# Windowed linear attention: left and right window borders passed by half blocks of four columns instead of whole blocks of eight

## Chip, cores and metric

One core of one Trainium2 chip. Time is device microseconds of one execution; the time of a kernel is the median of its runs.

## What is computed

An image of 256 channels and 64 x 64 pixels goes through three layers. The change is in the first, a linear attention over windows, with 8 heads of 32 channels and three window sizes:

```python
q = sigmoid(Wq x);  k = sigmoid(Wk x);  v = (Wv x) / |Wv x|     # x after a group norm
Ik  = integral(k);  Ikv = integral(k v^T)                       # sums over all rows above, columns to the left
for w in (1, 2, 4):                                             # windows of 64, 32 and 16 pixels
    attn = q . box(Ikv, 64 // w)                                # sum of k v^T over a window round each pixel
    norm = q . box(Ik, 64 // w)
    outs.append(attn / (norm + 1e-6))
x = x + Wout concat(outs) + bout
```

A window that leaves the image is cut at its edge. The second layer is a causal attention over the 4096 pixels as tokens (with layer norms and two dense layers), the third a mixture of experts of which two are computed.

## The kernel before

The k v sums of a window are never formed for each pixel. The image is cut into blocks of 8 x 8 pixels. `HALF` is half a window, 8, 16 or 32 pixels; `wi` counts them. For `wi` 1 and 2 a window of a query block has three kinds of keys:

- **Inside:** whole blocks that lie in the window of all queries of a block. Their k v sums come from two-dimensional running sums over blocks, `ikv`; `states` (L480) takes differences of these for a block row Y, ScalarE spreads them to block-diagonal matrices `bd` over four heads (L498), and `inside` (L404) multiplies them with q: for each of 8 blocks and 4 heads one product with 128 rows, 32 output columns and 64 queries (L409).
- **Left and right** (`beside`, L127): key blocks n columns to the left and right, of which each query column takes some key columns. The product of keys and queries is formed, blocked pairs are set to zero, and the rest is multiplied with v. `BLOCKED` (-64) is added for them by a small bf16 product of a row table and a column table (L348), and a ReLU takes the sum to zero.
- **Above and below** (`above`, L140): the same with rows; for `wi` 0 it is the whole window.

A `Part` is one tile of 128 keys with a rectangle of query rows and columns. `packed` (L105) fills lists of up to 512 query positions with parts; a part is split at a row where the piece has at least 96 positions. `push` (L337) takes a list: mask products (L348) and score products (L357) of four heads into four PSUM banks, the four heads on four groups of 32 rows of the PE array; then ReLU copies to SBUF, 5 of 8 on ScalarE (L326), 3 of 8 on VectorE (L328). One list later `add` (L369) multiplies with v (L390, 128 rows, 32 output columns, four heads side by side) into an accumulator. Accumulators of the left-and-right pass belong to a pair (`wi`, X), with two PSUM buffers for them; `store` (L397) copies a full one and writes it to HBM, and the up-and-down pass loads it by rows (L669) and adds it in `finish` (L415).

All this is done for each half of the heads (`hg` 0 and 1). A half goes through:

- four strips of 16 image rows: `project` (q and k, and k's running sum along rows), `values` (v, and its way to HBM and back in row order as `vh`), and from the second strip on `block_sums` (L580) of the strip before: k v sums of each block, 8 blocks x 2 x 4 heads as products of 64 keys;
- the left-and-right pass (L632 to L659), with `block_sums` of the last strip behind its first list;
- the up-and-down pass (L665 to L690): for each block row Y its lists, with `states`, `boxes` and `norms` (window sums of k and their product with q, for the next Y), `spread_norms`, `convolve` of Y-1, and in the second half `causal.norm` and `causal.turn` of Y-1 (layer norm of tokens for the second layer) at fixed places of the list's count.

What sets the order: inside `tc.manual_schedule` the instructions of PE and GpSimd run in the order in which the program issues them; for ScalarE, VectorE and the DMA queues a scheduler orders them[...]. GpSimd's order during the left-and-right pass is written out at L636 to L654: running sums of `ikv`, running sums of `ik` over 64 rows, `boxes(0)`, the reordering of k to `kh`, and for `hg` 0 the addition of a bias to the tokens `t`; `boxes(1)` follows from the loop over Y.

In the second layer `behind` (L921) forms sums over tokens, in tiles that `Causal.load` (L800) takes from the memory of `ik`; the rows of 128 queries are taken from the last to the first, with the dense layers' steps of finished groups (`later`) put between their products by `one()` (L1108 to L1148).

## Time and profile before

| what | us |
|---|---|
| median of 3 runs | 2015.45 (2014.27 to 2017.11) |
| the profiled execution's own time | 2017.58 |
| its span, first to last instruction | 2015.9 |
| strips, first half of the heads (41 to 92.7) | 51.7 |
| left-and-right pass, first half (92.7 to 203.6) | 110.9 |
| up-and-down pass, first half (203.6 to 516) | 312.4 |
| strips, second half (516 to 577.9) | 61.9 |
| left-and-right pass, second half (577.9 to 689) | 111.1 |
| up-and-down pass, second half (689 to 1032) | 343.0 |
| causal attention (1032 to 1748) | 716.0 |
| its end and the choice of experts (1748 to 1788) | 40.0 |
| experts (1788 to 2016) | 228.0 |

Engines are PE (TensorE; PEld its weight loads), DVE (VectorE), ACT (ScalarE), POOL (GpSimd) and SP (SyncE, which only issues DMAs here). "L390" is line 390 of the kernel. A row of the timeline has the start in us, the time until the last of its instructions ends, engine, line, operation, the tiles written and read, their shapes and the count; in square brackets the idle time of the engine before it and what ended that. Of a product, "32\*128 32x192" means weights of 32 rows and 128 columns with 192 columns moving. Consecutive rows of PE overlap[...]: the next row's start tells when the array took it. In a row of a group, the count is followed by busy time, the mean time of one in ns, and idle time before.

### The profile page before, as it was taken

To read this page: it belongs to the slowest core of one execution; us is meant where nothing else is said; L and a number is where in the kernel's file an instruction comes from. 1 tells how busy PE (TensorE), PEld (TensorE's weight loads), DVE (VectorE), ACT (ScalarE), POOL (GpSimd) and SP (SyncE) were. 2 spreads that over 40 slices of the span, in tenths; PEclk is the share of its full clock that TensorE was granted. 3 is DMA by queue.
4 is the path that set the end of the run, shared out by engine and by line. 5 is a ranking of instruction groups with operands and counts; after the bars stand their busy time and mean duration, and the time that the engine had idled before them with its cause. 6 is when DMAs were issued, how large, how long until landed. Compare 5 with 4: busy or idle time off the path is not lost.

```text
span 2015.9 us, 46364 instructions
## 1 busy us (share of the span) xinstructions
PE 1862.9 (92%) x20326; PEld 1224.0 (61%) x20326; DVE 985.5 (49%) x2190; ACT 829.0 (41%) x1459; POOL 431.2 (21%) x709
## 2 busy tenths in 40 slices
PE   4999899999999999898899999999999999879998
PEld 2655565555665565555574765666666666547787
DVE  4644444544554465555463434554554555433343
ACT  0566555554356654554413323332333233223322
POOL 1384322232155122333110000000000000021220
PEclk9999999999999999999999999999999999979999
DMA  7211000000331100000200000000000000010000
GB/s 239 80 52 50 23 13 16 15 18 13 96 98 40 44 18 13 18 13 12 49 2 0 0 1 0 1 1 0 1 0 1 0 1 0 1 42 21 21 21 21
DMA packets 66891, 53.35 MB, mean 26 GB/s; under 512 B 37568, under 2 KB 56792, under 8 KB 66688
## 3 DMA queue, kind: packets, MB, share of 16 engines
q1 hardware_dynamic: 57296, 31.87, 5.8%
q10 hardware_dynamic: 8128, 14.67, 2.1%
q0 software_dynamic: 1264, 3.84, 0.6%
q8 instruction: 159, 2.61, 0.5%
q14 instruction: 44, 0.36, 0.1%
HBM read 32.93 MB, written 17.44 MB: 25 GB/s over the span
## 4 chain that ended last, share of the span: by engine, by line
PE 42%; DVE 6%; ACT 3%; issue 2%; POOL 0%; ACTq 0%; DVEq 0%; POOLq 0%
PE po L1000 11%; PE pa L956 9%; PE ph L1260 6%; PE py L1280 5%; PE pt L986 2%; PE pm L1057 1%; PE acc L390 1%; PE pm L1067 1%; PE ps L357 1%; PE ps L507 1%; DVE lnst L704 1%; DVE sT L989 1%; DVE nbs L964 1%; PE pm L916 1%; ACT s L969 1%
## 5 line engine op out<-in xcount | busy, mean ns | idle before, releaser
L326 ACT ACTIVATE pm<-ps 128x512 f32<-128x512 f32 (+19 forms) x734 | 362.6, 559 | 320.3 <-issue 164.9
L328 DVE TENSOR_SCALAR pm<-ps 128x512 f32<-128x512 f32 (+23 forms) x442 | 267.8, 636 | 291.6 <-PE ps L357 210.8
L390 PE MATMUL acc<-pm,vh 128*32 128x248 f32 (+22 forms) x3424 | 220.1, 359 | 19.8 <-DVE pm L328 19.6
L357 PE MATMUL ps<-q,kh 32*128 32x248 f32 (+23 forms) x3424 | 209.8, 360 | 0.0
L956 PE MATMUL pa<-k,qT 128*128 128x512 f32 (+3 forms) x416 | 180.2, 574 | 7.1 <-ACT qT L918 5.7
L348 PE MATMUL ps<-table,table 32*128 32x192 bf16 (+19 forms) x2512 | 146.1, 262 | 39.3 <-DVE pm L328 18.4
L989 DVE COPY sT<-pt 128x512 f32<-128x512 f32 (+3 forms) x144 | 92.7, 643 | 138.1 <-PE pt L986 137.9
L348 PEld LDWEIGHTS <-table 32*128 32x128 bf16 x2512 | 51.0, 92 | 179.7 <-issue 172.8
L390 PEld LDWEIGHTS acc<-pm,vh 128*32 128x32 f32 x3424 | 88.9, 111 | 110.3 <-issue 63.2
L357 PEld LDWEIGHTS ps<-q,kh 32*128 32x128 f32 x3424 | 146.2, 192 | 7.5 <-issue 2.7
L425 POOL TENSOR_TENSOR y<-y,rn 128x512 f32<-128x512 f32 x32 | 40.8, 1275 | 477.5 <-DVE y L424 335.0
L958 ACT ACTIVATE s<-pa,v 128x512 f32<-128x512 f32 (+3 forms) x112 | 73.8, 662 | 148.6 <-PE pa L956 148.4
L956 PEld LDWEIGHTS pa<-k,qT 128*128 128x128 f32 x416 | 75.7, 191 | 89.3 <-issue 72.4
L964 DVE TENSOR_REDUCE nbs<-s 128x1 f32<-128x512 f32 (+4 forms) x120 | 77.6, 652 | 82.7 <-ACT s L958 58.9
L1280 PE MATMUL py<-w,hT 128*128 128x256 f32 x512 | 111.8, 379 | 0.0
L1000 PE MATMUL po<-kh,sT 128*128 128x257 f32 x406 | 101.3, 390 | 9.0 <-DVE sT L989 8.9
L1280 PEld LDWEIGHTS py<-w,hT 128*128 128x128 f32 x512 | 97.3, 190 | 15.7 <-issue 1.9
L390 PE MATMUL acc<-pm,v 128*32 128x192 f32 (+11 forms) x1600 | 98.5, 360 | 2.4 <-DVE pm L328 2.4
L357 PE MATMUL ps<-q,k 32*128 32x192 f32 (+11 forms) x1600 | 98.7, 359 | 0.7 <-issue 0.7
L1000 PEld LDWEIGHTS po<-kh,sT 128*128 128x128 f32 x406 | 73.7, 193 | 22.6 <-DVE sT L989 13.8
L507 PE MATMUL ps<-l0wo,y 128*128 128x256 f32 x384 | 87.2, 384 | 0.0
L947 POOL MEMSET s<- 128x32 f32 x20 | 2.5, 125 | 376.2 <-PE pt L986 348.4
(305 smaller groups left out, 2946.2 us busy)
## 6 DMA issues: line engine op xcount, KB each, us to landing
oscratch<-ov ACTq DMA_DIRECT2D x32, 256.0 KB
ov<-oscratch SPq DMA_DIRECT2D x32, 256.0 KB
t<-in_xT SPq DMA_DIRECT2D x32, 128.0 KB
vscratch<-v SPq DMA_DIRECT2D x32, 128.0 KB
vh<-vscratch SPq DMA_DIRECT2D x16, 256.0 KB
raw<-in_x ACTq DMA_DIRECT2D x7, 512.0 KB
raw<-in_x SPq DMA_DIRECT2D x7, 512.0 KB
out<-y SPq DMA_DIRECT2D x7, 512.0 KB
```

The costliest lines, as they stand in the source:

```text
L326: nc.scalar.activation(dst, src, AF.Relu)
L328: nc.vector.tensor_scalar_max(dst, src, 0.0)
L348: nc.tensor.matmul(got[h][:, spot].rearrange("p (y x) -> p y x", y=part.r1 - part.r0), lhsT=spread[hs, int(part.vertical), :], rhs=bias[hs ...
L357: nc.tensor.matmul(got[h][:, spot].rearrange("p (y x) -> p y x", y=part.r1 - part.r0), lhsT=keys[hs], rhs=q[hs, part.r0 : part.r1, part.c0 ...
L390: nc.tensor.matmul(out, lhsT=v, rhs=pm[:, h, spot].rearrange("p (y x) -> p y x", y=part.r1 - part.r0), start=fresh, stop=(left[key] == 0), ...
L507: nc.tensor.matmul(pt[:, i * D : (i + 1) * D], lhsT=ys[wi, Y][:, (2 * j + i) * P : (2 * j + i + 1) * P], rhs=wo[:, n, :], start=(n == 0), ...
L956: nc.tensor.matmul(pp[:, 0:m], lhsT=qTs[g][:, c, i * P - g * 512 : n - g * 512], rhs=x[b // 512][c][:, 0:m], start=(c == 0), stop=(c == DC ...
L964: nc.vector.tensor_reduce(nbs[:, at : at + 1], s[:, b : b + m], AX.X, ALU.max)
L989: nc.vector.tensor_copy(sT[:, 0:full], pt[:, 0:full])
L1000: nc.tensor.matmul(acc, lhsT=sT[0:m, j * P : (j + 1) * P], rhs=rhs, start=(b == 0), stop=(m != P))
L1260: nc.tensor.matmul(ph, lhsT=w1v[:, e, c, f, :], rhs=x2[g][c], start=(c == 0), stop=(c == DC - 1))
L1280: nc.tensor.matmul(py, lhsT=hT[:, e, f, j * P : (j + 1) * P], rhs=w2v[:, e, f, :], start=(e + f == 0), stop=(e == 1 and f == FC - 1))
```

## The change

Blocks of keys of 8 x 8 are kept, but the order of pixels within a tile of 16 x 8 keys changes, so that its partitions 0 to 63 hold columns 0 to 3 and 64 to 127 columns 4 to 7. A part of the left-and-right pass then stands for two halves u: four key columns, with the four query columns that lie n blocks beside them. A tile's 128 x 8 columns of scores become 128 x 4 (three where the right side's first column has no key). What lies between moves to the inside sums, which are kept by four columns: `ikv` has 17 column places instead of 9.

- Score products: per half and head 32 rows x 64 columns of weights. Sum products: 64 rows x 32 columns, each half into an accumulator of its own, with `wi` 1 in the first 256 columns and `wi` 2 in the last. Both PSUM buffers so belong to one X. `store` makes four copies and two DMAs for each X; lists are packed for each X; parts may be split at 40 positions, in the up-and-down pass too.
- `inside`: 16 places x 4 heads, 32 rows x 32 columns of weights, 32 queries, straight from `st`; `bd` and `heads` as its scale are gone.
- `block_sums`: four quarters of 32 keys instead of two halves of 64.
- GpSimd's running sums of `ikv` come after the reordering to `kh`, and start with rows.
- The token statistics are taken at list 4 (`measure`), root and normalising at list 5.
- `after`, `sums` and `count` of the second layer leave the memory of `ik`; one query product is issued ahead of four value products; in the last large row every step is followed by a step of the dense layers.

```diff
@@ -113,7 +114,7 @@
-        if rows * (part.c1 - part.c0) >= 96:
+        if rows * (part.c1 - part.c0) >= 40:
@@ -126,15 +127,16 @@
-        c0 = 8 * X + (1 if side and X - n >= 0 else 0)
+        c0 = 8 * X + side
...
-            yield Part(wi, True, (m, kX), side, 8 * lo, 8 * hi, c0, 8 * X + 8,
-                       -8 * (2 * m - n + 1), -8 * X, (wi, X))
+            yield Part(wi, True, (m, kX), side, 8 * lo, 8 * hi, c0, 8 * X + 4,
+                       -8 * (2 * m - n + 1), -8 * X, (X,))
@@ -353,12 +357,13 @@
-            for h, hs in enumerate(hss):
-                nc.tensor.matmul(
-                    got[h][:, spot].rearrange("p (y x) -> p y x", y=part.r1 - part.r0),
-                    lhsT=keys[hs], rhs=q[hs, part.r0 : part.r1, part.c0 : part.c1],
-                    start=False, stop=(i == len(parts) - 1), skip_group_check=True,
-                )
+            for u, some in enumerate(halves if part.vertical else whole):
+                for h, hs in enumerate(hss):
+                    nc.tensor.matmul(
+                        got[h][some, spot].rearrange("p (y x) -> p y x", y=part.r1 - part.r0),
+                        lhsT=keys[hs, some], rhs=q[hs, part.r0 : part.r1, part.c0 + 4 * u : part.c1 + 4 * u],
+                        start=False, stop=(i == len(parts) - 1), skip_group_check=True,
+                    )
@@ -372,56 +377,64 @@
-                accs[key] = po.tile([P, 512], F32, name="acc")
+                accs[key] = [po.tile([P, 512], F32, name="acc") for _ in (halves if part.vertical else whole)]
...
-                    inside(group, accs[key])
+                    inside(group, accs[key][0])
...
-            for h, hs in enumerate(hss):
-                if part.vertical:
-                    out = accs[key].rearrange("p (y x) -> p y x", x=8)[
-                        hs, part.r0 : part.r1, part.c0 % 8 : part.c0 % 8 + part.c1 - part.c0]
-                    v = state["v"][:, 8 * a_ + b_, hs]
-                else:
-                    out = accs[key].rearrange("p (y x) -> p y x", x=HW)[
-                        hs, part.r0 % 8 : part.r0 % 8 + part.r1 - part.r0, part.c0 : part.c1]
-                    v = vh[:, 4 * a_ + b_, hs]
-                nc.tensor.matmul(
-                    out, lhsT=v, rhs=pm[:, h, spot].rearrange("p (y x) -> p y x", y=part.r1 - part.r0),
-                    start=fresh, stop=(left[key] == 0), skip_group_check=True,
-                )
+            for u, some in enumerate(halves if part.vertical else whole):
+                for h, hs in enumerate(hss):
+                    if part.vertical:
+                        out = accs[key][u][:, 256 * part.wi - 256 : 256 * part.wi].rearrange("p (y x) -> p y x", x=4)[
+                            hs, part.r0 : part.r1, part.c0 % 8 : part.c0 % 8 + part.c1 - part.c0]
+                        v = state["v"][some, 8 * a_ + b_, hs]
+                    else:
+                        out = accs[key][0].rearrange("p (y x) -> p y x", x=HW)[
+                            hs, part.r0 % 8 : part.r0 % 8 + part.r1 - part.r0, part.c0 : part.c1]
+                        v = vh[:, 4 * a_ + b_, hs]
+                    nc.tensor.matmul(
+                        out, lhsT=v, rhs=pm[some, h, spot].rearrange("p (y x) -> p y x", y=part.r1 - part.r0),
+                        start=fresh, stop=(left[key] == 0), skip_group_check=True,
+                    )
...
-        wi, X = group
-        o = two.tile([P, 512], F32, name="ov")
-        nc.scalar.copy(o, acc)
-        nc.scalar.dma_start(out=oscratch[wi][X], in_=o)
+        X = group[0]
+        for wi in (1, 2):
+            o = sm.tile([P, 2, 64, 4], F32, name="ov", tag="y", bufs=4)
+            c = 0 if X >= HALF[wi] // 8 else 1
+            if c:
+                nc.vector.memset(o[:, :, :, 0:1], 0.0)
+            for u in range(2):
+                nc.scalar.copy(o[:, u, :, c:], acc[u][:, 256 * wi - 256 : 256 * wi].rearrange("p (y x) -> p y x", x=4)[:, :, c:])
+            nc.scalar.dma_start(out=oscratch[wi][2 * X : 2 * X + 2].rearrange("u p n -> p u n"),
+                                in_=o.rearrange("p u y x -> p u (y x)"))
...
-        for X in range(8):
+        for X in range(16):
...
-                    acc.rearrange("p (y x) -> p y x", x=HW)[hs, :, 8 * X : 8 * X + 8],
-                    lhsT=state["bd"][wi][:, X, h, :], rhs=q[:, 8 * Y : 8 * Y + 8, 8 * X : 8 * X + 8],
+                    acc.rearrange("p (y x) -> p y x", x=HW)[hs, :, 4 * X : 4 * X + 4],
+                    lhsT=state["st"][wi][hs, X, :], rhs=q[hs, 8 * Y : 8 * Y + 8, 4 * X : 4 * X + 4],
...
-        wi, Y = group
+        (wi, Y), acc = group, acc[0]
...
-            view = lambda s: s.rearrange("p (y b x) -> p y b x", b=8, x=8)
-            nc.vector.tensor_add(view(o), view(acc), state["ov"][wi].rearrange("p b (y x) -> p y b x", x=8))
+            view = lambda s: s.rearrange("p (y b x) -> p y b x", b=16, x=4)
+            nc.vector.tensor_add(view(o), view(acc), state["ov"][wi].rearrange("p b (y x) -> p y b x", x=4))
@@ -483,20 +496,21 @@
-            rows = state["h"].tile([P, 9, 32], F32, name="srows")
-            nc.vector.tensor_sub(rows, ikv[:, min(8, Y + n), :, :], ikv[:, max(0, Y - n + 1), :, :])
-            st = state["h"].tile([P, 8, 32], F32, name="st8")
-            if n == 2:
-                nc.vector.tensor_copy(st[:, 0, :], rows[:, 2, :])
-                nc.vector.tensor_sub(st[:, 1:7, :], rows[:, 3:9, :], rows[:, 0:6, :])
-                nc.vector.tensor_sub(st[:, 7, :], rows[:, 8, :], rows[:, 6, :])
+            hi, lo = min(8, Y + n) - 1, max(0, Y - n + 1) - 1
+            rows = ikv[:, hi, :, :]
+            if lo >= 0:
+                rows = state["h"].tile([P, 17, 32], F32, name="srows")
+                nc.vector.tensor_sub(rows, ikv[:, hi, :, :], ikv[:, lo, :, :])
+            st = state["h"].tile([P, 16, 32], F32, name=f"st{wi}")
+            n *= 2
+            nc.scalar.copy(st[:, 0:n, :], rows[:, n : 2 * n, :])
+            if n == 4:
+                nc.vector.tensor_sub(st[:, n : 17 - n, :], rows[:, 2 * n : 17, :], rows[:, 1 : 18 - 2 * n, :])
+                nc.vector.tensor_sub(st[:, 17 - n :, :], rows[:, 16:17, :].to_broadcast([P, n - 1, 32]),
+                                     rows[:, 18 - 2 * n : 17 - n, :])
...
-                nc.vector.tensor_copy(st[:, 0:4, :], rows[:, 4:8, :])
-                nc.vector.tensor_sub(st[:, 4:8, :], rows[:, 8:9, :].to_broadcast([P, 4, 32]), rows[:, 1:5, :])
-            bd = state["h"].tile([P, 8, 4, 32], F32, name=f"bd{wi}")
-            for h in range(4):
-                nc.scalar.activation(bd[:, :, h, :], st, AF.Copy, scale=heads[:, 32 * h : 32 * h + 1])
-            out.append(bd)
+                nc.vector.tensor_sub(st[:, n:, :], rows[:, 16:17, :].to_broadcast([P, n, 32]), rows[:, 1 : n + 1, :])
+            out.append(st)
@@ -557,10 +571,12 @@
-                nc.sync.dma_start(
-                    out=vscratch[2 * m + s].rearrange("(y b x) j e -> b y x j e", b=2, x=8)[b],
-                    in_=v[64 * s : 64 * s + 64, 8 * m : 8 * m + 8, :].rearrange("p (j b) e -> b p j e", b=2)[b],
-                )
+                for u in range(2):
+                    nc.sync.dma_start(
+                        out=vscratch[2 * m + s].rearrange("(y b u x) j e -> b u y x j e", b=2, u=2, x=4)[b, u],
+                        in_=v[64 * u + 32 * s : 64 * u + 32 * s + 32, 8 * m : 8 * m + 8, :].rearrange(
+                            "p (j b) e -> b p j e", b=2)[b],
+                    )
@@ -578,26 +594,26 @@
-        halves = [psum() for _ in range(2)]
+        quarters = [psum() for _ in range(4)]
...
-            for s in range(2):
-                px = slice(64 * s, 64 * s + 64)
+            for i in range(4):
+                px = slice(32 * i, 32 * i + 32)
...
-                    nc.tensor.matmul(halves[s][hs, 32 * X : 32 * X + 32], lhsT=kp[px, X, hs],
+                    nc.tensor.matmul(quarters[i][hs, 32 * X : 32 * X + 32], lhsT=kp[px, X, hs],
...
-        for s in range(2):
+        for i in range(4):
+            u, s = i // 2, i % 2
...
-                ikv[:, 1 + 2 * m + s, 1:, :], halves[s][:, 0:256].rearrange("p (b e) -> p b e", e=32))
+                ikv[:, 2 * m + s, 1:, :].rearrange("p (b u) e -> p u b e", u=2)[:, u],
+                quarters[i][:, 0:256].rearrange("p (b e) -> p b e", e=32))
...
-            two = vctx.enter_context(tc.tile_pool(name="l0v2", bufs=2, side="right", reuse_waits="tile"))
...
-            nc.gpsimd.memset(ikv[:, 0, :, :], 0.0)
-            nc.gpsimd.memset(ikv[:, 1:, 0, :], 0.0)
+            nc.gpsimd.memset(ikv[:, :, 0, :], 0.0)
@@ -629,25 +645,23 @@
-            lists = packed(part for X in range(8) for wi in (1, 2) for part in beside(wi, X))
+            lists = [parts for X in range(8) for parts in packed(part for wi in (1, 2) for part in beside(wi, X))]
...
-            for i in range(2, 9):
-                nc.gpsimd.tensor_add(ikv[:, 1:, i, :], ikv[:, 1:, i, :], ikv[:, 1:, i - 1, :])
-            for i in range(2, 9):
-                nc.gpsimd.tensor_add(ikv[:, i, :, :], ikv[:, i, :, :], ikv[:, i - 1, :, :])
...
-                    for b in range(2):
-                        nc.gpsimd.tensor_copy(
-                            kh[:, 8 * m : 8 * m + 8, :].rearrange(
-                                "p (s j) (y b x) -> p s b j y x", s=2, y=8, b=2)[:, s, b],
-                            k[:, m, :].rearrange("p (j b s y x) -> p s b j y x", j=4, b=2, s=2, y=8)[:, s, b],
-                        )
+                    nc.gpsimd.tensor_copy(
+                        kh[:, 8 * m : 8 * m + 8, :].rearrange("p (s j) (y b x) -> p s b j y x", s=2, y=8, b=4)[:, s],
+                        k[:, m, :].rearrange("p (j b s y x) -> p s b j y x", j=4, b=4, s=2, y=8)[:, s],
+                    )
+            for i in range(1, 8):
+                nc.gpsimd.tensor_add(ikv[:, i, 1:, :], ikv[:, i, 1:, :], ikv[:, i - 1, 1:, :])
+            for i in range(2, 17):
+                nc.gpsimd.tensor_add(ikv[:, :, i, :], ikv[:, :, i, :], ikv[:, :, i - 1, :])
@@ -677,10 +691,12 @@
-                    state.update(bd=bd, ov=ov, rn=spread_norms(r))
+                    state.update(st=st, ov=ov, rn=spread_norms(r))
...
+                    causal.measure(Y - 1)
+                if hg and i == 5 and Y:
@@ -821,14 +837,13 @@
-        self.after = take([NT, D + 1])
-        self.sums = take([P, DC, NT])
-        self.count = take([NT, 1])
+    def measure(self, g):
+        for i in range(4 * g, 4 * g + 4):
+            statistics(self.nc, self.low, self.t[:, i, :], self.stats[:, i, :])
...
-        for i in range(4 * g, 4 * g + 4):
-            statistics(nc, self.low, self.t[:, i, :], self.stats[:, i, :])
@@ -920,7 +936,8 @@
-            sums, count = causal.sums, causal.count
+            sums = sm.tile([P, DC, NT], F32, name="behind", bufs=1)
+            count = sm.tile([NT, 1], F32, name="count", bufs=1)
@@ -1110,8 +1127,8 @@
+            need(larges[0])
...
-            need(larges[0])
@@ -1134,6 +1151,10 @@
+                if r == len(larges) - 1:
+                    while todo:
+                        todo.pop(0)()
+                        one()
```

More of the change, by code (lines that the diff above doesn't have):

```diff
@@ L45, in window_tables @@
         spread[r, 0] = p // 16 == r
-        spread[r, 1] = p % 8 == r
+        spread[r, 1] = (p // 64 == r // 4) & (p % 4 == r % 4)
     for r in range(16):
@@ L49, in window_tables @@
     for r in range(2):
-        spread[8 + r, 1] = p // 64 == r
+        spread[8 + r, 1] = p // 32 % 2 == r
     out = [spread]
@@ L67, in window_tables @@
         n = half // 8
-        b = np.zeros((32, 2, 16 * n, 8), np.float32)
-        kx, rx = np.arange(8)[:, None], np.arange(8)[None]
+        b = np.zeros((32, 2, 16 * n, 4), np.float32)
+        kx, rx = np.arange(8)[:, None] % 4, np.arange(4)[None]
         for s, inx in enumerate((kx >= rx, kx < rx)):
@@ L235, in blocks @@
             )
-        heads = w.tile([P, P], F32, name="heads")
+        heads = sm.tile([P, P], F32, name="heads", tag="box", bufs=3)
         blocks(heads, 32, 1.0)
-        groups = w.tile([P, P], F32, name="groups")
+        groups = sm.tile([P, P], F32, name="groups", tag="box", bufs=3)
         blocks(groups, 8, 0.125)
@@ L281, in window_attention @@
                          (w, big, work, sm, dram, po), (spread, biases, sides),
-                         (heads, sums, spreadh, eps6, bo, going), late, causal)
+                         (sums, spreadh, eps6, bo, going), late, causal)
         with tc.manual_schedule(engines={mybir.EngineType.PE}):
@@ L287, in window_attention @@
                 f()
+            causal.measure(7)
             xns = causal.norm(7, w)
@@ L297, in window_heads @@
     spread, biases, sides = tables
-    heads, sums, spreadh, eps6, bo, going = consts
+    sums, spreadh, eps6, bo, going = consts
     oc = slice(hg * P, (hg + 1) * P)
@@ L314, in window_heads @@
     vscratch = dram.tile([8, P, 4, P], F32, name="vscratch")
-    oscratch = [None] + [dram.tile([8, P, 512], F32, name=f"oscratch{wi}") for wi in (1, 2)]
+    oscratch = [None] + [dram.tile([16, P, 256], F32, name=f"oscratch{wi}") for wi in (1, 2)]
     ik = causal.iks.tile([P, HW + 1, HW + 1], F32, name="ik")
-    ikv = big.tile([P, 9, 9, 32], F32, name="ikv")
+    ikv = big.tile([P, 8, 17, 32], F32, name="ikv")
     counter = [0]
@@ L330, in window_heads @@
     accs, left, state, ys, waiting = {}, {}, {}, {}, []
+    whole, halves = [slice(0, P)], [slice(0, 64), slice(64, P)]
     def expect(lists):
@@ L524, in project @@
                     nc.scalar.activation(
-                        q[:, 16 * m : 16 * m + 16, 32 * b : 32 * b + 32].rearrange("p y (b x) -> p b y x", x=8),
-                        pp.rearrange("p (b y x) -> p b y x", y=16, x=8), AF.Sigmoid)
+                        q[:, 16 * m : 16 * m + 16, 32 * b : 32 * b + 32].rearrange("p y (b x) -> p b y x", x=4),
+                        pp.rearrange("p (b y x) -> p b y x", y=16, x=4), AF.Sigmoid)
         rows = ik[:, 1 + 16 * m : 17 + 16 * m, :]
-        nc.gpsimd.tensor_copy(rows[:, :, 1:].rearrange("p y (b x) -> p b y x", x=8),
-                              k[:, m, :].rearrange("p (b y x) -> p b y x", y=16, x=8))
+        nc.gpsimd.tensor_copy(rows[:, :, 1:].rearrange("p y (b x) -> p b y x", x=4),
+                              k[:, m, :].rearrange("p (b y x) -> p b y x", y=16, x=4))
         for s in range(2):
@@ L612, in normalise @@
                             nc.vector.tensor_scalar(
-                                g[:, c, :].rearrange("p (b j h s y x) -> p b s h j y x", b=2, j=2, h=2, s=2, y=8)[:, b, s],
-                                raw[:, c, :].rearrange("p (s b j y h x) -> p b s h j y x", s=2, b=2, j=2, y=8, h=2)[:, b, s],
+                                g[:, c, :].rearrange("p (b j h s y x) -> p b s h j y x", b=2, j=2, h=4, s=2, y=8)[:, b, s],
+                                raw[:, c, :].rearrange("p (s b j y h x) -> p b s h j y x", s=2, b=2, j=2, y=8, h=4)[:, b, s],
                                 gm, rs, op0=ALU.subtract, op1=ALU.mult,
@@ L667, in window_heads @@
             for wi in (1, 2):
-                o = h.tile([P, 8, HW], F32, name=f"ov{wi}")
-                nc.sync.dma_start(out=o, in_=oscratch[wi].rearrange("b p (y x) -> y p b x", x=HW)[Y])
+                o = h.tile([P, 16, 32], F32, name=f"ov{wi}")
+                nc.sync.dma_start(out=o, in_=oscratch[wi].rearrange("b p (y n) -> y p b n", n=32)[Y])
                 ov.append(o)
-            bd = states(Y)
+            st = states(Y)
             if hg and Y == 7:
@@ L885, in __init__ @@
                                 pattern=[[1, NE], [-1, NE]], channel_multiplier=0)
+        self.after = tile("after", [NT, D + 1])
         self.stats = tile("stats2", [P, NT, 2])
@@ L900, in causal_attention @@
         causal.rest(big)
-        x, v, stats, after = causal.x, causal.v, causal.stats, causal.after
+        x, v, stats, after = causal.x, causal.v, causal.stats, given.after
         mm, mb, wt, col, row = causal.mm, causal.mb, causal.wt, causal.col, causal.row
```

## Prediction

> **What bounds the kernel now.** I read the shares of the page first, then stretches of the span, then the timeline of TensorE (PE) and GpSimd (POOL) inside the stretches that the change touches, and last the idle time ahead of single PE instructions.

> ```profile
> PE 1862.9 (92%) x20326; PEld 1224.0 (61%) x20326; DVE 985.5 (49%) x2190; ACT 829.0 (41%) x1459; POOL 431.2 (21%) x709
> ```

> PE is busy for 92%. By stretch (length; then busy time and count of PE, PEld, DVE, ACT, POOL; granted clock, DMA share, GB/s):

> ```profile
> 92.70:203.60 110.90, 106.72 (x2119) 62.56 (x2118) 50.82 (x80) 68.77 (x135) 72.11 (x127) 1.00 0.16 51
> 203.60:516.00 312.40, 290.82 (x5571) 180.18 (x5572) 150.44 (x273) 165.68 (x348) 88.11 (x106) 0.98 0.07 16
> 577.90:689.00 111.10, 108.02 (x2122) 63.28 (x2120) 50.72 (x80) 68.73 (x136) 53.46 (x119) 0.98 0.15 50
> 689.00:1032.00 343.00, 307.40 (x5635) 191.47 (x5634) 186.91 (x386) 170.99 (x362) 87.41 (x103) 0.96 0.08 20
> 1748.00:1788.00 40.00, 19.79 (x61) 12.28 (x61) 22.27 (x86) 8.80 (x25) 7.15 (x9) 0.64 0.15 48
> ```

> Rows one and three are the left-and-right pass of each half of the heads: 111 us, PE busy for 107. PE sets their length; in the first POOL is busy for 72 us of it. Rows two and four are the up-and-down passes. One list of that pass:

> ```profile
> 106.64 1.07 PE L390 MATMUL acc<-pm,v 128*32 128x256 f32 x16
> 107.64 0.37 PE L348 MATMUL ps<-table,table 32*128 32x192 bf16 x8
> 107.85 0.93 PE L357 MATMUL ps<-q,k 32*128 32x192 f32 x16
> 108.70 1.07 PE L390 MATMUL acc<-pm,v 128*32 128x192 f32 x16
> 109.71 0.39 PE L348 MATMUL ps<-table,table 32*128 32x256 bf16 x7
> ```

> Start to start: 0.21 us masks, 0.85 scores, 1.01 sums. Two parts of 512 columns give 16 f32 instructions, so each f32 product is two, run in rounds of four (one per head). Read one by one in the trace, a round of 232 columns takes 196 ns, 168 take 143, 224 take 189: **0.85 ns a column**, two rounds a part. Rounds of 105 columns take 101 to 111 ns instead of 89[...]. Between L357 and L390, and back, about 90 ns pass after the last column.

> [...]eight 64x32 tiles in the block sums (next fence), whose first 40 matmuls start within 163 ns, 33 ns per tile and turn, so that rows 0-63 and 64-127 overlap. [...]nothing in this trace has several row tiles writing one bank.

> **The pass itself.** Parts shrink from 8 (or 7) query columns to 4 (or 3). Counted over the eight column blocks: before, 46 lists, 100 parts, 22,592 columns; after, 24 lists, 96 parts, 10,080 columns. Per half of the heads, in us:
> - Before: masks 22,592 x 0.42 ns = 9.4; scores 39.6 and sums 39.0 (two rounds a part, 0.85 ns a column, at least 104 ns for scores): 88.0. The other 22.9: 46 lists x 2 mode changes x 0.09 = 8.3; block sums with waits 3.4; norms 1.0; two waits 2.0; left 8.2, or 0.18 a list, short waits for banks.
> - After, if both halves run side by side: masks 4.2; scores 18.4, sums 17.9 = 40.5. Mode changes 24 x 3 x 0.09 = 6.5 (masks stay 32x128, scores become 32x64, sums 64x32); banks 24 x 0.18 = 4.3; block sums 4.5; norms and waits 3. An odd half-round at a phase's end: 0 to 4, I take 2. Both accumulators now belong to one column block, so that the next block's sums wait for ScalarE's copies: 2.5 evictions ahead (1.4 us) and three or four copies of 128x256 (0.36 us each by L589) against 1.5 to 2.2 us of PE work: 0 to 1.4 per block, I take 0.7 x 8 = 5.6. Sum **66.4**.

> That is 44.5 saved per half: **-89**. Eviction keeps its ratio, 512 columns a list; the copies and two stores per block cost ScalarE 1.44 us instead of 1.2.

> **Block sums and inner sums.**

> ```profile
> 90.50 1.29 PE L586 MATMUL ps<-v,kp 64*32 64x32 f32 x128
> L409 PE MATMUL acc<-q,bd 128*32 128x64 f32 x2048 | 35.2, 222 | 0.0
> ```

> L586 doubles to 256 instructions. After the burst two start every 16.7 ns; at that pace 128 more cost 1.07 us; if sixteen tiles overlap better, 0.5. I take 1.0: three calls ahead of the pass, **+6** over both halves (the fourth is above). L409 goes from 64 matmuls (14 ns each, 0.90 us) to 128 of 32 columns on four diagonal tiles: at 33 ns a tile turn, or 8.35 ns an instruction, 1.07 us. Its mode becomes 32x32 between sums of 128x32: two changes, 0.18. So +0.35 x 32 = **+11**; bounds 0[...] and the last rival.

> **POOL, whose cover shrinks.**

> ```profile
> 98.58 5.56 POOL L637 TENSOR_TENSOR ikv<-ikv 128x256 f32<-128x256 f32 x7 [5.90 <-DVE ikv L589]
> 104.22 6.05 POOL L639 TENSOR_TENSOR ikv<-ikv 128x288 f32<-128x288 f32 x7
> 110.22 25.03 POOL L641 TENSOR_TENSOR ik<-ik 128x64 f32<-128x64 f32 x63
> 144.93 5.54 POOL L646 COPY kh<-k 128x256 f32<-128x256 f32 x16
> 150.43 18.71 POOL L654 TENSOR_TENSOR t<-t,l0bo 128x1024 f32<-128x1024 f32 x8
> 196.74 0.24 POOL L443 COPY box<-rows 128x64 f32<-128x64 f32 x1 [26.35 <-PE ps L461]
> ```

> The last line's 26 us of idle time is the cover. Let S be the start of the pass. POOL can begin at S-1: ik 25.0, boxes 9.7, kh 5.5 (same elements in half the instructions), then ikv, moved behind these: 7 x 1.28 (as L453's 512 elements) + 15 x 0.79 (as L637) = 20.9. kh is ready at S+39, needed at S+66; ikv at S+60, needed by the first inner sums at about S+82. In the first half t's 18.7 and the next boxes (10.4) follow: S+89. PE wants those boxes for its norms 25 us after the pass (203.6 to 228.6 now), at S+90. **Cost 0, but no cover is left**: each further us on POOL there is lost. The second half has no t adds: S+70 against S+90.

> **What else moves.**

> ```profile
> 212.32 0.33 PE L348 MATMUL ps<-table,table 32*128 32x168 bf16 x8 [2.47 <-ACT rn L476]
> 959.16 0.06 DVE L924 MEMSET ik<- 128x2 f32 x1 [9.82 <-POOL rows L440]
> 959.90 0.36 PE L348 MATMUL ps<-table,table 32*128 32x248 bf16 x4 [6.48 <-DVE pm L328]
> 1759.58 1.67 PE L1090 MATMUL pt<-ident,att 128*128 128x128 f32 x6 [6.24 <-DVE att L1082]
> ```

> - The 128 weighted copies bd on ScalarE (54.9 us in all) go. Only at row 0 of each half do they stand ahead of rn (2.47 us, twice): **-4** (0 to -8). VectorE's state sums keep about their size.
> - L924's memset waits for POOL's last read of ik, evictions behind it, PE behind those. In its own tile it no longer does: **-6.5**. If the new tile inherits another late owner, 0.
> - Statistics stay at list 4; square root, reciprocal and normalising (0.30 and 0.18 + 1.38 us) come at list 5. ScalarE now waits 48 us there (7 times), with evictions behind it, and PE then loses up to 1.55 us. I take **-3** (-8 to +3: PE's transposes at list 7 keep two lists, about 4 us, for the rest).
> - In the last large row each step of the late layers is followed by attention work: of the 6.24 us perhaps 4 are covered: **-4** (0 to -6); then the 4.03 us wait of the last tile is next. The query product moved ahead of four value products hides its eviction, which no wait shows now: 0.
> - The finer split leaves the up-and-down pass 96 lists and 248 parts instead of 101 and 214: five fewer lists x 0.36 us against 34 parts x some 50 ns: 0 (-3 to +5).
> - SP issues 8 stores of v a strip instead of 4 (0.69 us each); vh, queued behind, is read some 60 us later: 0. The loads of ov have 128-byte instead of 256-byte runs; 0, as ov is read 20 us after its issue (208.5 to 228.1) while DMA is 7% busy.

> Sum: -89 + 6 + 11 - 4 - 6.5 - 3 - 4 = **-89.5**. The profiled execution took 2017.6 us (span 2015.9), 2.1 above the median 2015.45 of the runs: 2015.5 - 89.5 = **1926**.

> **Rivals.**
> - POOL becomes the bound. Runs of four elements may make its ikv sums and kh copies slower; at twice their time, 26.4 us more, the first half's norms wait 25.6 and the second's some 7: **1958**. For: no cover; against: its strided rows show about the same time per element.
> - The halves take turns, both using the same rows of the array for scores: scores and sums last twice as long, +36.3 - 2 per half: **1994**. Against: the block sums' overlap; for: no 32x64 tile is in the trace.
> - Slower: the four diagonal tiles of the inner sums take turns at their one bank. 128 x 33 ns = 4.2 us instead of 1.07, 32 times: +101, **2027**. It decides from 30 ns a matmul on (89.5 / 32 + 1.07 = 3.87 us over 128). [...]for: every other row-tiled product here has a bank per row tile.

> **Chances.** Forecast 0.70 (its own range 1900 to 1950), POOL 0.13, turns of the halves 0.07, turns at the bank 0.06, mixtures 0.04. Low end: inner sums at no cost (-11), no waits at blocks and no odd round in the second half (-8; the first is held by POOL), the small gains at their ends (-9): 1898, rounded to 1895. High end: the POOL case and bank waits twice as long: 1965. A measurement of this kernel can tell 0.2%, some 4 us, from no change. Faster 0.90 (forecast, POOL, halves), within 0.2% 0.02, slower 0.08.

> **What would show it.** Right: passes of some 66 us; eight scores starting within about 30 ns; inner sums of 1.1 to 1.3 us; no PE gap ahead of the norms of row 1; none of 6 us near the last row of the second half. Wrong: a PE wait for POOL's box there; inner sums over 2 us; score rounds of twice 0.85 ns a column.

## The result, and the profile after

The changed kernel takes 2044.28 us (median of 4 runs, 2040.83 to 2048.2) against 2016.28 for the kernel before on the same chip (4 runs): ratio 1.014, 95% interval 1.0118 to 1.0161. It is **slower by 1.4%**, where 1926 and faster was forecast. The profiled execution took 2043.33 (span 2041.6), 25.7 us of span more than before.

The share of PE after, and the stretches that answer to those of before (length; busy time and count of PE, PEld, DVE, ACT, POOL; granted clock, DMA share, GB/s):

```profile
PE 1834.8 (90%) x27670; PEld 1270.9 (62%) x27670; DVE 958.4 (47%) x2084; ACT 726.1 (36%) x1269; POOL 449.0 (22%) x707
```

```profile
39.80:105.00 65.20, 59.83 (x996) 41.00 (x997) 38.05 (x67) 28.45 (x46) 19.10 (x25) 0.93 0.28 74
105.00:213.40 108.40, 78.81 (x3691) 59.41 (x3694) 25.87 (x45) 36.00 (x91) 78.18 (x120) 0.85 0.15 48
213.40:534.00 320.60, 302.02 (x7301) 203.09 (x7298) 157.47 (x244) 144.80 (x292) 86.83 (x103) 0.99 0.11 19
609.50:718.80 109.30, 77.43 (x3687) 58.75 (x3686) 25.87 (x46) 36.03 (x91) 58.24 (x109) 0.85 0.15 48
718.80:1059.60 340.80, 313.14 (x7368) 210.45 (x7355) 192.39 (x355) 149.53 (x305) 89.59 (x106) 0.99 0.12 22
1059.60:1773.00 713.40, 681.99 (x2750) 453.30 (x2750) 350.50 (x914) 224.95 (x283) 39.44 (x135) 0.99 0.00 1
```

| stretch | before | after | difference |
|---|---|---|---|
| strips, both halves | 51.7 + 61.9 | 65.2 + 75.5 | +27.1 |
| left-and-right passes | 110.9 + 111.1 | 108.4 + 109.3 | -4.3 |
| up-and-down passes | 312.4 + 343.0 | 320.6 + 340.8 | +6.0 |
| causal attention | 716.0 | 713.4 | -2.6 |

In the passes (rows two and four) PE's busy time falls by 28 and 31 us and the length hardly at all: PE stands still for 30 of 108 us in the first, where it had been 4 of 111. What it waits for, first in the timeline of PE in the first pass, then in the groups of PE (idle time ahead, and what ended it):

```profile
133.78 1.20 PE L362 MATMUL ps<-q,k 32*64 32x9 f32 x78
135.99 0.61 PE L362 MATMUL ps<-q,k 32*64 32x120 f32 x18 [1.01 <-issue]
136.53 1.21 PE L397 MATMUL acc<-pm,v 64*32 64x96 f32 x80
137.68 0.37 PE L352 MATMUL ps<-table,table 32*128 32x51 bf16 x12
137.98 0.47 PE L362 MATMUL ps<-q,k 32*64 32x51 f32 x17
139.91 0.75 PE L362 MATMUL ps<-q,k 32*64 32x168 f32 x31 [1.46 <-issue]
140.59 1.33 PE L397 MATMUL acc<-pm,v 64*32 64x9 f32 x96
141.85 0.21 PE L352 MATMUL ps<-table,table 32*128 32x96 bf16 x1
143.64 0.41 PE L352 MATMUL ps<-table,table 32*128 32x96 bf16 x19 [1.58 <-issue]
```

```profile
L362 PE MATMUL ps<-q,k 32*64 32x96 f32 (+17 forms) x3072 | 70.8, 295 | 24.3 <-issue 24.2
L397 PE MATMUL acc<-pm,v 64*32 64x96 f32 (+17 forms) x3072 | 64.0, 285 | 19.3 <-issue 14.6 <-DVE pm L331 3.3 <-ACT pm L329 1.3
L422 PE MATMUL acc<-q,st 32*32 32x32 f32 x4096 | 42.7, 193 | 5.9 <-issue 5.9
L602 PE MATMUL ps<-v,kp 32*32 32x32 f32 x2048 | 22.8, 211 | 20.4 <-issue 19.5 <-ACT pm L329 1.0
```

Before, the scores and sums of these passes and the block sums hardly waited on "issue" at all:

```profile
L357 PE MATMUL ps<-q,k 32*128 32x192 f32 (+11 forms) x1600 | 98.7, 359 | 0.7 <-issue 0.7
L390 PE MATMUL acc<-pm,v 128*32 128x192 f32 (+11 forms) x1600 | 98.5, 360 | 2.4 <-DVE pm L328 2.4
L586 PE MATMUL ps<-v,kp 64*32 64x32 f32 x1024 | 10.8, 204 | 2.3 <-ACT pm L326 2.3
```

"issue" means that nothing in the profile held PE. The gap at 139.91 breaks into the middle of one list's scores (17 products, gap, 31 products), whose banks its mask products (L352) had already written, so no eviction and no buffer can be its cause. The gaps recur at 135.99, 139.91 and 143.64: every 3.7 to 3.9 us. Between two gaps lie 127 and 128 products (the counts of the rows): with as many weight loads, 256 instructions. The DMA view shows something else in that rhythm: queue q8, kind "instruction", with packets of 16,384 bytes, that is 64 bytes for each of 256 instructions. Its row for 130 to 145 us, before and after:

```profile
q8 instruction: 2, 0.03, 1.0%
```

```profile
q8 instruction: 4, 0.07, 1.9%
```

The queue's count fits PE over the whole execution: 27,670 products and as many loads are 55,340 instructions, or 216.2 times 256, and q8 has 216 packets (before: 40,652, 158.8 and 159). And the gaps follow the packets: each of the 22 "issue" gaps over 0.3 us in the first pass ends 1.2 to 1.6 us after a packet has landed.

Start to start, the packets of the changed kernel's first pass lie 3.42 to 4.38 us apart, median 3.69. Before, the median in the pass was 6.58, and the smallest distance in the whole execution 3.43. The theory (A): **PE's instructions arrive in packets of 256, one per 3.4 to 3.7 us at best, some 14 ns an instruction and 28 ns for a pair of load and product. The pass issues 7385 instructions; at 14.2 ns (3.64 us a packet) that is 105 us, however short each product is.** Rivals: B, the halves or the small tiles take turns on the array; C, evictions and stores; D, GpSimd.

### The profile page after: what moved, and what is told of

Read it like the earlier page. It is cut to its first block, busy times and chain, and to the rows that moved or that the text cites. A ratio compares the mean times of both kernels' runs of the same rounds, so it can differ in the third digit from the quotient of the medians.

```text
span 2041.6 us, 60741 instructions
## 1 busy us (share of the span) xinstructions
PE 1834.8 (90%) x27670; PEld 1270.9 (62%) x27670; DVE 958.4 (47%) x2084; ACT 726.1 (36%) x1269; POOL 449.0 (22%) x707
## 4 chain that ended last, share of the span: by engine, by line
PE 46%; DVE 7%; ACT 3%; issue 2%; POOL 0%; ACTq 0%; DVEq 0%; POOLq 0%
PE po L1017 11%; PE pa L973 9%; PE ph L1281 6%; PE py L1301 5%; PE pt L1003 2%; PE acc L397 2%; PE ps L362 2%; PE ps L521 2%; PE pm L1074 1%; PE pm L1084 1%; DVE lnst L720 1%; PE ps L352 1%; DVE sT L1006 1%; DVE nbs L981 1%; PE pm L932 1%
## 5 line engine op out<-in xcount | busy, mean ns | idle before, releaser
L329 ACT ACTIVATE pm<-ps 128x502 f32<-128x502 f32 (+15 forms) x600 | 295.2, 556 | 396.7 <-PE ps L362 183.6
L331 DVE TENSOR_SCALAR pm<-ps 128x502 f32<-128x502 f32 (+15 forms) x360 | 220.3, 643 | 353.2 <-PE ps L362 225.9
L397 PE MATMUL acc<-pm,vh 128*32 128x192 f32 (+24 forms) x3968 | 216.2, 328 | 14.6 <-DVE pm L331 14.2
L362 PE MATMUL ps<-q,kh 32*128 32x192 f32 (+24 forms) x3968 | 213.0, 335 | 3.4 <-issue 3.3
L362 PEld LDWEIGHTS ps<-q,kh 32*128 32x128 f32 x3968 | 162.4, 187 | 16.3 <-issue 8.0
L397 PEld LDWEIGHTS acc<-pm,vh 128*32 128x32 f32 x3968 | 102.1, 110 | 91.2 <-issue 35.7
L352 PE MATMUL ps<-table,table 32*128 32x184 bf16 (+29 forms) x2752 | 118.1, 239 | 30.4 <-ACT rn L489 9.3
L973 PEld LDWEIGHTS pa<-k,qT 128*128 128x128 f32 x416 | 75.3, 190 | 89.5 <-issue 72.4
L352 PEld LDWEIGHTS <-table 32*128 32x128 bf16 x2752 | 50.7, 93 | 120.8 <-issue 113.6
L1017 PE MATMUL po<-kh,sT 128*128 128x257 f32 x406 | 102.7, 394 | 8.7 <-DVE sT L1006 8.5
L362 PE MATMUL ps<-q,k 32*64 32x96 f32 (+17 forms) x3072 | 70.8, 295 | 24.3 <-issue 24.2
L1017 PE MATMUL po<-v,sT 128*128 128x257 f32 x342 | 81.6, 380 | 0.0
```

Source lines behind the costliest of these rows:

```text
L329: nc.scalar.activation(dst, src, AF.Relu)
L331: nc.vector.tensor_scalar_max(dst, src, 0.0)
L352: nc.tensor.matmul(got[h][:, spot].rearrange("p (y x) -> p y x", y=part.r1 - part.r0), lhsT=spread[hs, int(part.vertical), :], rhs=bias[hs ...
L362: nc.tensor.matmul(got[h][some, spot].rearrange("p (y x) -> p y x", y=part.r1 - part.r0), lhsT=keys[hs, some], rhs=q[hs, part.r0 : part.r1 ...
L397: nc.tensor.matmul(out, lhsT=v, rhs=pm[some, h, spot].rearrange("p (y x) -> p y x", y=part.r1 - part.r0), start=fresh, stop=(left[key] == ...
L973: nc.tensor.matmul(pp[:, 0:m], lhsT=qTs[g][:, c, i * P - g * 512 : n - g * 512], rhs=x[b // 512][c][:, 0:m], start=(c == 0), stop=(c == DC ...
```

## Experiments

"Before" beside a time is the kernel before on the same chip. Lengths of passes are from the first to the last score product (before 105.8 and 106.1, after 102.9 and 105.8).

**Half of the instructions, all the columns.**

```diff
-                for h, hs in enumerate(hss):
+                for h, hs in enumerate(hss[0:2] if part.vertical else hss):
...
-                for h, hs in enumerate(hss):
+                for h, hs in enumerate([slice(0, 64), slice(64, P)] if part.vertical else hss):
```

> The changed kernel; in the left-and-right pass the scores are made for heads 0 and 1 only, and the sums for those two with weights of 64 columns (two heads' values, so every row of the accumulators is still written). It leaves out the scores of heads 2 and 3 and half of their sums. The passes keep their lists, columns, evictions and stores; 16 of a part's 32 score and sum matmuls go. Heads lie on different rows of the array, so a round of the array should be no shorter. Theory A (PE gets its instructions at some 14 ns each, 256 per 3.6 us): about 2200 pairs are left of 3690, so the pass falls from 108 to 63-68 us of PE time; it then also tests the forecast of GpSimd, whose boxes end 89 us after the pass begins, so that the pass may end at 90-95. Total 2000 to 2015 (both halves 30 to 40 shorter, less the waits for GpSimd). Theory B (the two halves, or the tiles of 64 rows, take turns on the array): the pass stays at 104-108, total 2035-2045.

Measured: 1999.37 (before 2009.75). The first pass fell to 67.3, the second to 96.2 only. The two passes' stretches:

```profile
105.30:173.50 68.20, 60.88 (x2145) 48.55 (x2144) 24.27 (x42) 36.90 (x90) 61.91 (x104) 0.89 0.23 74
575.30:672.00 96.70, 94.24 (x2142) 74.47 (x2130) 26.71 (x46) 37.55 (x89) 56.73 (x107) 0.50 0.16 52
```

In the second, PE is busy for 94 of 97 us, at a granted clock of 0.50. To see whether that belongs to the pass, the kernel ran again:

> The kernel with scores of heads 0 and 1 only, again, with more runs (it leaves out the scores of heads 2 and 3 and half of their sums). In its first run the first pass took 67 us at a granted clock of 0.89, the second 96 us at 0.50, from the first to the last score. If the low clock goes with the sparse work of such a pass by chance, one or both passes may come at another clock now: a pass at a clock over 0.85 takes 64-70 us, one at 0.50 some 90-100, and times spread over some 30 us, 1965 to 2005. If the second pass is held by something else (GpSimd's boxes, the stores), it takes 90-100 us again at whatever clock.

Measured: 1979.61 (4 runs, 1966.68 to 1985.51), ratio to before 0.9817 (0.9768 to 0.9866). In the profiled run the second pass is now the fast one (66.3), and the first (82.1) has the lower clock, 0.62:

```profile
105.30:187.60 82.30, 78.64 (x2130) 63.63 (x2118) 23.62 (x41) 37.01 (x89) 72.75 (x111) 0.62 0.19 61
587.20:653.70 66.50, 61.29 (x2126) 48.90 (x2118) 23.71 (x41) 36.71 (x89) 54.04 (x102) 0.90 0.23 75
```

So the slow pass goes with the clock (66.3 and 67.3 us at 0.90 and 0.89, 82.1 at 0.62, 96.2 at 0.50) and not with its place. B as turns of the halves falls: the columns and rounds stayed and the pass went from 103 to 67. No PE wait for GpSimd's boxes shows in either run, so D falls as well.

**All the instructions, under half of the columns.** Each product takes only the rows of its own band:

```diff
+        lo, hi = max(0, 16 * m - part.r0), min(n, 16 * m + 16 - part.r0)
...
-                        lhsT=keys[hs, some], rhs=q[hs, part.r0 : part.r1, part.c0 + 4 * u : part.c1 + 4 * u],
+                        lhsT=keys[hs, some], rhs=q[hs, part.r0 + lo : part.r0 + hi, part.c0 + 4 * u : part.c1 + 4 * u],
...
```

> The changed kernel; in the left-and-right pass every score and sum matmul is still issued, but with only the query rows of its own 16-row band, some 40% of the columns (a part without such rows does one row). It leaves out the rest of the scores and sums. Instructions, lists, bias matmuls, evictions and stores stay. Theory A (instruction supply): the pass stays within 105-109 us, total 2038-2048. Theory B (array time, halves in turns or slow small tiles): array time of scores and sums falls by over half, the pass to 60-75, total 1970-1990 unless GpSimd's boxes hold it at 90 (then 2005).

Measured: 2033.42 (before 2009.75); passes 104.4 and 102.7, where the changed kernel has 102.9 and 105.8. Their stretches:

```profile
104.70:214.00 109.30, 75.30 (x3707) 60.32 (x3710) 25.86 (x45) 36.37 (x91) 76.76 (x117) 0.53 0.15 48
606.50:714.00 107.50, 76.78 (x3706) 61.35 (x3699) 25.76 (x45) 36.39 (x91) 59.30 (x111) 0.50 0.15 49
```

The columns fell by over half, and the length stayed. The clock fell too, from 0.85 to 0.53 and 0.50, and PE's busy time hardly changed (75.3 and 76.8 us, against 78.8 and 77.4 in the changed kernel); so the length alone would not rule the array out. The waits do: PE stands still for 34 and 31 us of these stretches, most of it on "issue", and the packets are 3.73 and 3.72 us apart (median), as in the changed kernel at a higher clock. The array does not set the length.

**The same bound put into the kernel before.** Each sum product is cut into four by rows; no halves, the same columns.

> The kernel before; in its left-and-right pass each sum matmul is cut into four by query rows, the same columns in all, the same tiles of the array, no halves: 398 in place of 100 parts times 4 heads times 2 passes of f32. Nothing is left out. Theory A: the pass needs about 4500 pairs at 28.4 ns = 128 us in place of 111, with issue gaps every 3.6 us as in the changed kernel; total 2045-2055. Theory B: only halves or 64-row tiles are slow; the pass stays at 111-116, total 2016-2026.

Measured: 2127.65 (before 2009.75), passes 160.4 and 160.3, far over both theories. The cut was badly ordered: the four pieces of one head followed each other on the same 32 columns of the array, 96 ns apart at 112 columns, so heads no longer ran side by side. Packets came 4.56 us apart: not the supply. With the heads inside:

```diff
+            for lo, hi in zip(cuts[:-1], cuts[1:]):
+                for h, hs in enumerate(hss):
```

> As the cut sums before, with the order mended: of the four pieces of a part, the four heads' matmuls of one piece follow each other, so that they lie on four column groups of the array and run side by side, as uncut; in the first version the four pieces of one head, all on the same column group, followed each other and waited in turn (96 ns from start to start for 112 columns), which is no question of supply. Nothing is left out. Theory A: about 8760 instructions in the pass at 14.2 ns give 124-130 us in place of 106 between its first and last score, with packets 3.5 to 4 us apart; total 2040-2055. Theory B: 106-116, total 2010-2025.

Measured: 2058.63 (before 2013.16), 4 us over A's range; passes 130.6 and 127.4, around the upper end of A's 124 to 130, packets 3.73 and 3.62 apart, at full clock:

```profile
92.00:226.00 134.00, 113.01 (x4393) 85.51 (x4392) 49.53 (x79) 68.75 (x135) 70.50 (x125) 0.99 0.13 42
L393 PE MATMUL acc<-pm,v 128*32 128x48 f32 (+9 forms) x6368 | 111.5, 217 | 26.3 <-issue 22.8 <-DVE pm L328 3.4
```

**The supply by itself.** Six streams, nothing else:

```diff
+    nc.tensor.matmul(banks[r][32 * c : 32 * c + 32, 0:n], lhsT=w[32 * r : 32 * r + 32, i % 16, 32 * c : 32 * c + 32],
+                     rhs=x[32 * r : 32 * r + 32, 0:n], start=True, stop=True, skip_group_check=True)
```

> A kernel of its own that computes nothing of the reference: six streams on PE of 1024 pairs of weight load and matmul each, on constant data, each ended by a short copy on VectorE: (1) tiles of 32 by 32, 16 places of the array in turn, 8 columns, bf16; (2) the same with 64 columns; (3) and (4) the same two in f32, 512 matmuls of two passes each; (5) 128 by 128, 8 columns, bf16; (6) 128 by 128, 64 columns, bf16. Theory A (instructions come in packets of 256, one per 3.4 to 3.7 us, whatever they do): streams 1 to 4 all take 27 to 30 us, 28 ns for a pair, with no difference between 8 and 64 columns, in bursts faster than 20 ns for a pair broken by issue gaps of 0.5 us and more at intervals of 3.6 us; 5 and 6 take no less. Rival (each small matmul has its own cost of some 28 ns on the array or at issue): the starts are evenly spaced, 25 to 30 ns, without gaps. Theory B (array time): streams 2 and 4 are slower than 1 and 3.

Measured, first to last start over 1023: 25.1, 28.5, 27.6 and 28.1 ns a pair for the small tiles with 8 bf16, 64 bf16, 8 f32 and 64 f32 columns (the first stream begins with packets already there); 29.2 and 30.9 for the large ones. Second stream:

```profile
29.69 1.11 PE L174 MATMUL bank<-xb,wb 32*32 32x64 bf16 x95 [0.26 <-DVE o L184]
32.81 1.27 PE L174 MATMUL bank<-xb,wb 32*32 32x64 bf16 x128 [2.01 <-issue]
36.54 1.27 PE L174 MATMUL bank<-xb,wb 32*32 32x64 bf16 x128 [2.46 <-issue]
40.54 1.27 PE L174 MATMUL bank<-xb,wb 32*32 32x64 bf16 x128 [2.73 <-issue]
```

Exactly 128 pairs in 1.27 us (8 ns from start to start), then over 2 us of nothing. The mean of 28 ns is no cost of a product; it is a burst and a wait. Each of the 31 restarts in the small streams comes 1.2 to 1.6 us after a packet has landed, and between 30 and 116 us nothing but these packets is on the DMA queues (24 in all), so no other transfer holds them up. The 128 x 128 stream of 8 columns has 27 ns from start to start and is almost as slow by itself: the supply hardly shows there.

**Block sums with fewer instructions.** First with one product in place of four:

```diff
-                for hs in hss:
-                    nc.tensor.matmul(quarters[i][hs, 32 * X : 32 * X + 32], lhsT=kp[px, X, hs],
+                for hs in hss[0:1]:
+                    nc.tensor.matmul(quarters[i][:, 32 * X : 32 * X + 32], lhsT=kp[px, X, :],
```

> The changed kernel; the sums of k v by four columns are made with one matmul in place of four (all four heads' keys as weights, 128 columns, against the values of head 0), so 64 pairs of weight load and matmul for a call in place of 256. Every cell is still written, but for heads 1 to 3 with the product with head 0's values. Theory A: where PE waits for instructions a call is 192 pairs or 384 instructions shorter, 5.4 us; of these 8 calls some are covered, and the strips before the pass (65.2 and 75.5 us) go back to 52-56 and 62-66; total 2015-2025. Theory C (the strips grew because of the evictions of four quarters or the eight stores of values to DRAM): the strips stay above 62 and 72 us, total over 2035.

Measured: 2016.75 (before 2009.75). The strips of the first half:

```profile
39.80:96.40 56.60, 54.94 (x419) 36.73 (x419) 36.20 (x65) 27.52 (x45) 16.88 (x21) 1.00 0.29 83
```

65.2 went to 56.6, just over A's range; of the 13.5 us more than before, 8.6 go with the instructions of the block sums. The clock is 1.00 again, in place of 0.93, and the 8.6 hold its share. In the second half, from the last score of the up-and-down pass to the first of the left-and-right pass, the strips take 64.1 us before, 78.7 after and 66.2 here. What is left, 4.9 and 2.1 (four copies in place of two, eight stores in place of four, or the other shape of the products), stays open.

Then a form that leaves nothing out, 128 x 128 products of which the diagonal blocks are copied:

> The changed kernel; the sums of k v by four columns come from one matmul of all four heads' keys against all four heads' values, 128 by 128, of which only the four blocks on the diagonal are copied out: 64 pairs for a call in place of 256, and 32 copies of 128 columns on 32 rows in place of 4 of 256 columns on 128. Nothing is left out. Theory A: 5.4 us of supply go from each of 8 calls, against 2-4 us of copies on ScalarE and VectorE, partly beside PE: ratio to before 1.002 to 1.010 (2020-2036). Theory C (evictions set the strips): slower than the changed kernel, ratio over 1.016.

Measured: 2050.74 (4 runs), ratio to before 1.0171 (1.0143 to 1.02), no better than the changed kernel. PE's issue gaps ahead of the block sums are gone, and a wait for the copies has taken their place:

```profile
L602 PE MATMUL ps<-v,kp 32*128 32x128 f32 x512 | 34.3, 299 | 8.3 <-DVE ikv L607 8.3
L607 DVE COPY ikv<-ps 32x128 f32<-32x128 f32 x128 | 36.7, 286 | 2.5 <-PE ps L602 0.2
```

128 copies of 0.29 us on VectorE and as many on ScalarE cost at least as much as the supply they save. A's forecast for this kernel missed, and the ratio lies where C had put it: here the copies, eight times as many, do set the strips. For the changed kernel that does not follow; its block sums waited 19.5 us on "issue" and none on their copies.

**Inner sums by eight columns.**

```diff
-        for X in range(16):
+        for X in range(0, 16, 2):
```

> The changed kernel; the inner sums are made with 8 matmuls for a head and row in place of 16, each over 8 query columns (with the state of every other four columns, so the other states are left out). Half of 4096 matmuls and weight loads of that line go, the columns streamed stay. Theory A (supply): a row's call of 128 pairs is 256 instructions, one packet, 3.6 us at the sustained rate; 64 pairs fewer are 1.8 us for a call if PE waits for instructions there; the page shows only 5.9 us of issue gaps ahead of this line, so 10 to 25 us of the total go: 2015-2033. Rival (the calls lie inside what was already fetched): under 6 us, total 2034-2044.

Measured: 2027.98 (before 2013.16); its span is 15.3 us below that of the changed kernel (2026.3 and 2041.6). It is one run, and 16 runs of the kernel before lay between 2007.46 and 2020.86; the traces say more than the totals: from the last score of the left-and-right pass to their own last, the up-and-down passes are 6.3 and 7.7 us shorter. The gaps are gone and the busy time falls from 42.7 to 35.1:

```profile
L422 PE MATMUL acc<-q,st 32*32 32x64 f32 x2048 | 35.1, 216 | 0.0
```

**The changes of order alone**, on the kernel before (statistics, memory of `after`, `sums` and `count`, query product, last large row):

> The kernel before with only the changes of order that came along with the halves: the tokens' statistics measured one list ahead of their root, the buffers of behind() and of its result in memory that is free early, so that the memset ahead of the last row has nothing to wait for, the queries of the first large row ahead of values(7), and the remaining steps of the last large row one by one between the later work. Left-and-right pass, block sums and inner sums are those of before; nothing is left out. Theory A: these parts of the sum held (6.5 for the memset, 3 for the statistics, up to 4 for the last row), and the halves alone made the kernel slower: 5 to 13 us below before, ratio 0.9935 to 0.9975. Rival: the gain was taken from elsewhere (waits that moved), ratio 0.998 to 1.002.

Measured: 2005.65 against 2013.16, ratio 0.9963 (0.9948 to 0.9978). This version beats both kernels. If the two ratios (1.014 and 0.9963) add up, the halves alone cost 1.8%, some 36 us.

## Why the prediction was wrong, step by step

- **"After, if both halves run side by side: ... Sum 66.4" is the step that failed.** They do run side by side: at full clock eight scores of 128 columns start 109 ns after the eight before them, 0.85 ns a column, and in turns it would be twice that. But the sum had only the array's time, mode changes, banks, evictions and waits. It put the supply of instructions at nothing: 96 parts make 7385 of them with the block sums behind the first list, 105 us at 14.2 ns, and the passes took 108.4 and 109.3. Before, 4237 instructions in 110.9 us were one per 26 ns. -89 became -4.3. Where instructions were halved and the clock stayed high, the pass did take 66 to 67; that kernel lies near its own supply bound (4289 x 14.2 = 61 us), so the 66.4 is neither shown nor contradicted. The array's own term was somewhat low: eight scores of 51 columns take 97 ns, over twice the 43 ns of 0.85 ns a column, and with the rounds of the trace at full clock an estimate for scores and sums is 44 us in place of 36.3. Nor is 104 ns a floor for a round of scores before: it was read from rounds of 105 columns, while rounds of 88 and of 24 columns took 76 and 26 ns in the same trace; what holds the rounds of 105 at 101 to 111 ns was not shown, and the floor under the short rounds of the new form was the author's estimate.
- **"At that pace 128 more cost 1.07 us"** came from a call of 128 products, 256 instructions: just one packet, already there. The call is now 512 instructions, two packets: one runs from 81.60 to 85.15 us, with 1.05 us of gap in it, in place of 1.29. +6 became +27 in the strips; in those of the first half the clock was 0.93, before 1.00, and how much of the 27 that makes was not measured. A reading beside it was wrong too: within 163 ns the trace of before has 32 starts, four turns of eight tiles, and not 40. No term of the sum rests on it.
- **Inner sums, +11:** about right: 42.7 us busy and 5.9 idle in place of 35.2 is +13.4. A call without a gap takes 1.10 us from its first start to its last, where 1.07 was forecast, so no turns at one bank show (4.2). The 5.9 us of "issue" gaps are supply and were not in the sum.
- **bd, -4:** the waits of PE for rn fell from 13.0 to 9.3 us, those at row 0 from 2.47 to 0.27. Right.
- **The memset, -6.5:** right. The 6.48 us gap at L348 is in neither the changed kernel nor the one with only the order changed.
- **Statistics, -3:** nothing. Four times in the second half PE loses 1.55 us here before, 1.55 in the kernel with only the order changed, and still 1.48 in the changed one.
- **Last large row, -4:** 0.4. The 6.24 us wait became 3.45, and 2.43 moved to the step ahead:

```profile
1765.89 1.21 PE L1065 MATMUL pt<-ident,att 128*128 128x128 f32 x6 [2.43 <-DVE att L1057]
1785.57 1.67 PE L1107 MATMUL pt<-ident,att 128*128 128x128 f32 x6 [3.45 <-DVE att L1099]
```

- **POOL, 0 without cover:** held where it could be seen, in the 67 us pass; in the changed kernel the pass stayed long enough to cover everything.
- **The slower rival** had the right sign for a wrong reason. The case that came, a supply of instructions that binds once products are short, was in no rival. The trace of before had the hint: 159 packets on q8, never two within less than 3.43 us. At that distance the 29 packets that 7385 instructions need give 99 us.

## What to carry to other kernels

Before cutting products into smaller ones, count PE's instructions in the stretch (each product and each weight load, twice for f32 here) and multiply by the shortest distance per instruction that the instruction queue shows (3.43 us for 256 in the kernel before). Where that exceeded the forecast array time here, it was the better forecast, and still a low one: 99 us against 66.4, and passes of 108. A rate read inside one burst of up to 256 instructions said nothing of a longer run: 8 ns a pair in a burst of the second stream, 28.5 over its 1024 pairs. Idle time of PE marked "issue" that returned at one interval (3.7 to 3.9 us), in the middle of like products, was the sign.
